# Splitting the last sequence's slot softmax, taking variances from running sums, and re-ranking the last stages of a linear-attention and soft-MoE kernel

## The chip, the cores and the metric

The kernel runs on one core of a Trainium2 chip. A core has five engines that run side by side, each with its own in-order queue: TensorE (PE; its weight loads are shown apart as PEld), VectorE (DVE), ScalarE (ACT), GpSimd (POOL) and SyncE (SP), which here issues the DMA transfers. The metric is the device time of one execution in microseconds (us). Lower is better.

## The reference

The input x holds 4 sequences of 2048 tokens with 256 channels, float32. One layer of linear attention and one soft mixture of experts follow each other, each with a residual and a layer norm behind it:

```python
q, k, v = (gelu(x @ W1 + b1) @ W2 + b2 for each of q, k, v)
scores = tril(q @ k.T / scale)              # no softmax
a = layernorm(scores @ v) * ln_w + ln_b
x = layernorm(x + a)

xn = layernorm(x) * ln_gamma + ln_beta
logits = (xn / norm(xn)) @ (mu / norm(mu))  # 16 experts x 16 slots = 256 columns
dispatch = softmax(logits, over the 2048 tokens of a sequence)
combine = softmax(logits, over the 256 slots)
slot_in = dispatch.T @ xn                   # 256 slots x 256 channels, per sequence
slot_out = gelu(slot_in @ w1 + b1) @ w2 + b2    # per expert
x = layernorm(x + combine @ slot_out)
```

The softmax over the tokens ties a sequence together: no slot sum is final before the sequence's last logits are known, and no output of a sequence can be formed before its slot outputs.

## The kernel before

The 8192 tokens are cut into 16 groups of 512 tokens, four groups to a sequence; a group is four blocks of 128 tokens. For each group t the program states a series of steps, in three functions: `attend` (projections, causal attention with a carried state), `norms` (the two layer norms in front of the experts and the l2 norm) and `back` (logits, their minima over the tokens in `mx`, the softmax over slots, whose result is turned into `ct`). The sign of the logits is flipped, so minima stand for maxima. After the fourth group of a sequence come `softmaxes` (the shift over all tokens of the sequence: two transposes of `mx`, a reduction, a matmul that spreads the shift over all partitions, a copy `cmb` by ACT, then for each group a subtraction on POOL, L1158, and an exponential on ACT, L1167), `slots` and four times `finish`.

`slots` adds up the 16 blocks of a sequence in PSUM, for each half h of the 256 slots (L1182, which appears as two instructions a block and half, 64 a sequence), divides by the sum of the weights (`si`, L1191 and L1192), transposes (L1203), scales (`siT`, L1212), multiplies with w1 (L1227), copies and transposes again (L1237, L1246), applies the Gelu (`hz`, L1265), multiplies with w2 (L1273) and adds the bias (`so`, L1282). There is one tile `so` for all sequences. `finish` loads `ct` back (SP, four transfers), turns it on DVE, and for each block multiplies it with `so` (L1336, `combine`), adds the residual (L1360 on DVE; in the last sequence every second block by a copy on ACT, L1345, and an addition on POOL, L1352), takes mean and variance by bn_stats and bn_aggr (L536, L537), the root by a power on POOL (L525), a product of two small columns on DVE (L563), centers and scales the block (L574 on ACT, L579 on DVE) and stores the group through SP (L1320). The last group is stored in two halves.

The order in each engine's queue is not the order of statement. A planner (`Plan`) gives every step a length and a rank. It runs a small model of the engines, takes in turn the step that can begin earliest, and where several of one engine can begin at the same time, the one of lowest rank. The rank is a base, set by `plan.begin`, that counts groups (a step that reads PSUM gets 1.5 less). The bases of group t are t for `attend`, t+0.6 for `norms`, t+1.1 for `back`; of a sequence whose last group is t, t+1.4 for `softmaxes`, t+1.7 for `slots`, t+2.6 and up for `finish`. For the third sequence alone `slots` has a rank above all others, so that its matmuls fill what PE has left over:

```python
late = 100.0 if b == B - 2 else 0.0
plan.begin(t + 1.7 + (100.0 if late else 0.0))
so = slots(b)
for i in range(NG):
    plan.begin(t + 2.6 + 0.2 * i + (3.5 if late else 0.0))
    finish(t - NG + 1 + i, so)
```

The emitted program is fixed: at run time each engine works through its queue in that order and waits where an operand is late. Tiles are named by tags with a fixed number of places; `dg` (diagonal and `cmb`) has one place, `cm` (shift) three, `root` sixteen, `xT` two, `lg` (logits) seven.

Of the kernel before, what the change touches and what calls it, by code (L numbers as in the profile page):

```python
# [14 lines left out]
P = 128  # L15
G = 4
LAST = 2
# [29 lines left out]
class Plan:  # L47
# [62 lines left out]
    def run(self):  # L110
# [25 lines left out]
        while left:  # L136
            best = None
            for e, steps in ready.items():
                chosen = None
                for s in steps:  # L140
# [4 lines left out]
                    if s.table and s.table != table[0]:  # L145
                        at += self.TABLE
                    key = (at + self.PATIENCE[e] * s.rank, s.rank, at)
# [60 lines left out]
def kernel(  # L208
# [41 lines left out]
    for tag, n, shape in (  # L250
# [23 lines left out]
        ("root", 16, [G]),  # L274
# [5 lines left out]
        ("cm", 3, [EH]),  # L280
# [259 lines left out]

    def variances(mv):
        return mv[:, :, 1:2].rearrange("p c o -> p (c o)")
# [46 lines left out]
    def spread(col, name):  # L589
# [19 lines left out]
    def unit_mu():  # L609
# [26 lines left out]
        row = spread(mr, "mu")  # L636
# [304 lines left out]
    def norms(t):  # L941
# [16 lines left out]
        st2, mv2 = plan.buffer("st", G), plan.buffer("mv", G)  # L958
        for c in range(G):

            def emit(c=c):
                nc.vector.scalar_tensor_tensor(
                    row[:, c, :C], a[:, c, :], r[:, c : c + 1], row[:, c, :C],
                    ALU.mult, ALU.add,
                )

            plan.step("DVE", 0.42, emit, [(a, [c]), r], [(row, [c])])
            means((row, [c]), st2, mv2, c, lambda c=c: row[:, c, :C])
        ve2, w2 = plan.buffer("ve"), plan.buffer("ve")
# [3 lines left out]
                w2.place, variances(mv2), 1.0 + LN_EPS, LN_EPS * LN_EPS, ALU.mult, ALU.add  # L973
            ),
            [mv2], [w2],
        )
        rr = inv_root(w2, G)
        center_on(row, mv2, rr, ("DVE", "ACT") * 2)
        plan.step(
            "DVE", 0.17,  # L980
            lambda: nc.vector.tensor_scalar_add(ve2.place, variances(mv2), LN_EPS),  # L981
# [5 lines left out]
        def emit():  # L987
# [6 lines left out]
        plan.step(  # L994
            "POOL", _pool(G * C),
            lambda: nc.gpsimd.tensor_tensor(
                by_halves(xn), row[:, :, :C].rearrange("p g (k d) -> p k g d", k=KC), gam_h,
                ALU.mult,
            ),
            [row], [xn],  # L1000
        )
        plan.step(
            "POOL", _pool(G * C),
            lambda: nc.gpsimd.tensor_tensor(by_halves(xn), by_halves(xn), bet_h, ALU.add),
            [], [xn],
        )
# [5 lines left out]
        for c in range(G):  # L1012

            def emit(c=c):
                nc.scalar.activation(
                    squares, by_halves(xn)[:, :, c, :], AF.Square,
                    accum_out=ss[:, c : c + 1],
                )
# [12 lines left out]
    def back(t):  # L1031
# [44 lines left out]
        first = t % NG == 0  # L1076
# [49 lines left out]
    def softmaxes(b):  # L1126
# [20 lines left out]
        row = spread(cm, f"cm_{b}")  # L1147
# [6 lines left out]
        for t in range(b * NG, (b + 1) * NG):  # L1154
            lg = l_tiles[t]
# [15 lines left out]
    def slots(b):  # L1171
# [23 lines left out]
        for t in ts_:  # L1195
            del l_tiles[t]
# [245 lines left out]
```

## Time and profile before

| | |
|---|---|
| median of 3 runs | 671.45 us (670.31 to 672.46) |
| the profiled execution | 673.21 us |
| its span, first to last instruction | 671.5 us |
| mean granted PE clock | 0.994 |
| PE busy | 648.3 us, 97% |
| PEld busy | 482.3 us, 72% |
| DVE busy | 499.5 us, 74% |
| ACT busy | 256.8 us, 38% |
| POOL busy | 296.1 us, 44% |

A stage table of the profile gives, for a stretch of the span, its length and the busy time of each engine in it with the number of instructions. From 584 us on, where the last group's attention is done, PE is busy 74.1 of 87.5 us, DVE 58.3, ACT 37.6 and POOL 34.1.

A line of the timeline gives start, length, engine, source line, operation, output and inputs, and how many such instructions are merged; in brackets stand the idle time of the engine before it and what ended it. A line of the chain of waits gives start, length, engine and source line, merged over neighbours of one kind.

### The profile page before, as it was taken

Reading aid. Unit: us, or ns where it says so; the run is one execution under the profiler, and the core shown is the slowest. Engines: PE = TensorE matmul, PEld = TensorE weight load, DVE = VectorE, ACT = ScalarE, POOL = GpSimd, SP = SyncE. Lnnn points to the kernel's source line nnn. Section 1 sums busy time; section 2 is a strip of 40 time slices with the busy share of each in tenths; the row PEclk is TensorE's granted clock in tenths of the full one; section 3 lists DMA queues with packets and bytes.
Section 4 is the critical chain, followed back from the end, with each engine's and each line's share of the span. In section 5 each row is a group of like instructions: output and inputs, shape, how many; then the busy total and the mean of one; then the engine's idle time right before and its main releaser. Section 6 shows DMA issues by size and latency. Waiting matters only on the chain.

```text
span 671.5 us, 9220 instructions
## 1 busy us (share of the span) xinstructions
PE 648.3 (97%) x2966; PEld 482.3 (72%) x2966; DVE 499.5 (74%) x1319; ACT 256.8 (38%) x540; POOL 296.1 (44%) x305
## 2 busy tenths in 40 slices
PE   6999999999999999999999999999999999999994
PEld 3757586776768877858676877767676868877873
DVE  1438586979797878869786488996877689967396
ACT  3130414334355326130626134623425543434346
POOL 4343616061648514361608307446153844543324
PEclk9999999999999999999999999999999999998998
DMA  8953655886667197637586345985586356100034
GB/s 245 254 119 106 133 94 132 127 159 142 118 139 122 44 176 188 176 82 139 131 127 125 63 95 145 214 189 104 120 156 133 76 113 95 55 1 0 32 95 156
DMA packets 311831, 82.59 MB, mean 123 GB/s; under 512 B 244716, under 2 KB 309544, under 8 KB 311784
## 3 DMA queue, kind: packets, MB, share of 16 engines
q1 hardware_dynamic: 310680, 80.96, 57.2%
q10 hardware_dynamic: 960, 0.80, 0.5%
q8 instruction: 23, 0.38, 0.3%
q0 software_dynamic: 144, 0.26, 0.1%
q14 instruction: 24, 0.20, 0.1%
HBM read 51.00 MB, written 30.99 MB: 122 GB/s over the span
## 4 chain that ended last, share of the span: by engine, by line
PE 91%; DVE 5%; issue 1%; DMA 1%; ACT 1%; POOL 0%; ACTq 0%; DVEq 0%
PE mm L720 24%; PE at L1182 8%; PE at L1336 8%; PE mm L1060 8%; PE at L822 8%; PE mm L770 8%; PE at L905 7%; PE mm L743 7%; PE at L795 4%; PE at L909 4%; PE at L855 1%; PE tp L469 1%; DVE st L536 1%; DMA row<-in_x_dram 1%; ACT row L574 1%
## 5 line engine op out<-in xcount | busy, mean ns | idle before, releaser
L525 POOL TENSOR_TENSOR root<-ve,nhalf 128x4 f32<-128x4 f32 (+1 forms) x49 | 50.6, 1033 | 157.4 <-DVE ve L981 56.8
L730 ACT ACTIVATE hid<-mm,cols_sb 128x512 f32<-128x512 f32 x96 | 65.1, 687 | 141.6 <-PE mm L720 141.1
L574 ACT ACTIVATE row<-row,root,root 128x256 f32<-128x256 f32 x94 | 49.9, 591 | 44.7 <-DVE root L563 44.6
L720 PE MATMUL mm<-xT,W1q_sb 128*128 128x512 f32 x128 | 61.5, 610 | 0.3 <-DVE xT L459 0.3
L905 PE MATMUL at<-state,hid 128*128 128x256 f32 x240 | 61.7, 379 | 0.0
L822 PE MATMUL at<-vt,kt 128*128 128x256 f32 x240 | 61.3, 385 | 0.0
L743 PE MATMUL mm<-both_sb,hid 128*128 128x257 f32 x256 | 59.5, 381 | 1.4 <-DVE kt L753 1.4
L1336 PE MATMUL at<-so,ct 128*128 128x256 f32 x256 | 58.3, 381 | 2.2 <-DVE so L1282 1.6
L720 PE MATMUL mm<-xT,W1v_sb 128*128 128x512 f32 x128 | 59.4, 592 | 0.0
L1060 PE MATMUL mm<-mu_sb,xnT 128*128 128x256 f32 x256 | 59.3, 385 | 0.0
L770 PE MATMUL mm<-W2v_sb,hid 128*128 128x256 f32 x256 | 58.2, 380 | 0.3 <-DVE kt L753 0.3
L720 PE MATMUL mm<-xT,W1k_sb 128*128 128x512 f32 x128 | 57.8, 593 | 0.0
L1182 PE MATMUL at<-row,lg 128*128 128x257 f32 x256 | 56.6, 379 | 0.0
L1110 POOL TENSOR_TENSOR sum<-sum,ss 128x4 f32<-128x4 f32 x16 | 3.8, 237 | 119.1 <-DVE ss L1106 102.5
L1336 PEld LDWEIGHTS at<-so,ct 128*128 128x128 f32 x256 | 47.8, 190 | 11.2 <-DVE so L1282 2.0
L1060 PEld LDWEIGHTS mm<-mu_sb,xnT 128*128 128x128 f32 x256 | 49.3, 194 | 8.7 <-issue 1.4
L743 PEld LDWEIGHTS mm<-both_sb,hid 128*128 128x128 f32 x256 | 48.2, 190 | 9.8 <-DVE kt L753 2.0
L536 DVE BATCH_NORM_STATS2 st<-row 128x6 f32<-128x256 f32 x128 | 53.5, 418 | 1.8
L905 PEld LDWEIGHTS at<-state,hid 128*128 128x128 f32 x240 | 45.5, 190 | 12.1 <-issue 5.7
L770 PEld LDWEIGHTS mm<-W2v_sb,hid 128*128 128x128 f32 x256 | 48.3, 190 | 7.5 <-DVE kt L753 0.9
L948 POOL TENSOR_TENSOR row<-row,rows_sb 128x1024 f32<-128x1024 f32 x16 | 35.2, 2204 | 41.8 <-DMA row<-in_x_dram 27.8
L1182 PEld LDWEIGHTS at<-row,lg 128*128 128x128 f32 x256 | 48.4, 190 | 7.1
(129 smaller groups left out, 1176.4 us busy)
## 6 DMA issues: line engine op xcount, KB each, us to landing
bounce<-xn SPq DMA_DIRECT2D x28, 512.0 KB
row<-in_x_dram SPq DMA_DIRECT2D x16, 512.0 KB
bounce<-kt SPq DMA_DIRECT2D x30, 256.0 KB
kT<-bounce SPq DMA_DIRECT2D x60, 128.0 KB
out_dram<-row SPq DMA_DIRECT2D x15, 512.0 KB
xT<-in_x_dram SPq DMA_DIRECT2D x112, 64.0 KB
xnT<-bounce SPq DMA_DIRECT2D x56, 128.0 KB
ct<-bounce SPq DMA_DIRECT2D x56, 128.0 KB
```

What stands on the lines that cost most here:

```text
L525: nc.gpsimd.tensor_tensor(r[:, :n], v[:, :n], nhalf.to_broadcast([P, n]), ALU.pow)
L536: nc.vector.bn_stats(st[:, c, :], access())
L574: nc.scalar.activation(dst[:, c, :C], dst[:, c, :C], AF.Identity, bias=nm[:, i : i + 1], scale=r[:, i : i + 1],)
L720: nc.tensor.matmul(ph.place, wa[f"W1{n}"][:, k, m * P : (m + 1) * P], xT[:, k, :], start=(k == 0), stop=(k == KC - 1),)
L730: nc.scalar.activation(hid[n][:, m, :], ph.place, AF.Gelu, bias=cols_sb[:, 4 * i + m : 4 * i + m + 1],)
L743: nc.tensor.matmul(pk[:, : C + 1], hid["k"][:, k, c * P : (c + 1) * P], wqk_sb[:, k, :], start=(k == 0), stop=(k == KC - 1),)
L770: nc.tensor.matmul(pv[:, j * C : (j + 1) * C], hid["v"][:, k, (c0 + j) * P : (c0 + j + 1) * P], wa["W2v"][:, k, :], start=(k == 0), stop=( ...
L822: nc.tensor.matmul(pds[:, m * C : (m + 1) * C], kt[:, c, m * P : (m + 1) * P], vt[:, c, :], start=True, stop=True,)
L905: nc.tensor.matmul(po[:, :C], qT[:, k, toks[c]], s[:, k, :], start=(k == 0), stop=False,)
L1060: nc.tensor.matmul(pl[:, j * ES : (j + 1) * ES], xnT[:, k, (c0 + j) * P : (c0 + j + 1) * P], mu_sb[:, k, :], start=(k == 0), stop=(k == KC ...
L1182: nc.tensor.matmul(psi[:, : C + 1], lg[:, c, h * P : (h + 1) * P], row[:, c, :], start=(i == 0 and c == 0), stop=(i == NG - 1 and c == G - 1),
L1336: nc.tensor.matmul(pc[:, :C], ct[:, h, c * P : (c + 1) * P], so_t[:, h, :], start=(h == 0), stop=(h == EH - 1),)
```

## The change

In the last sequence (groups 12 to 15):

- The softmax over the tokens is done in two parts. Behind group 14, `softmaxes` runs over groups 12 to 14 with the minima so far, and `part_sums` adds up their slot sums (24 calls of L1182's kind, 12 for each half) and copies them to SBUF (`kept`, in a place of `xT`). Group 15 has minima of its own. Its shift is the lesser of the two, its subtraction and exponential are done block by block (blocks 0 and 3 on POOL, 1 and 2 on DVE), its slot sums take 8 calls, and the kept sums are scaled by the exponential of the difference of the shifts and added.
- `norms` of group 15 has rank 15.0 instead of 15.6 and `back` 15.3 instead of 16.1. The scaling with gamma and beta of that group goes block by block, two blocks on POOL and two on DVE.
- The third sequence's `slots` has rank 15.6 instead of 112.7 and its four `finish` 16.5, 16.8, 17.1 and 17.4 instead of 17.1, 17.3, 17.5 and 17.7. The last sequence has 15.4 and 16.2 for the early softmax and the early sums, 15.5 for the late softmax (16.4 before), 16.7 for `slots`, and 17.6 to 17.9 for `finish` (17.6 to 18.2 before). The product with w2 is not planned before the tile `so` is free.

In groups 8 to 15 (`finish`) and 14 and 15 (the second layer norm in `norms`), the variance no longer comes from bn_stats. The addition on DVE hands out the row sum as well (`accum_out`), and ACT squares 256 times the difference from the mean, again with a row sum. POOL forms the root and the product with the mean by itself. The addition is on DVE for every block. Centering is on ACT for groups 8 to 10, and mostly on DVE from group 11 on.

The places of `root` go from 16 to 24, those of `cm` from 3 to 6. The new term with `TAIL["table"]` in the planner is zero with the value set, 1.0. The core of the diff:

```diff
+ACCZ = 14
+LASTN = 2
+CENTERS = (('ACT', 'ACT', 'ACT', 'ACT'), ('ACT', 'ACT', 'ACT', 'ACT'), ('ACT', 'ACT', 'ACT', 'ACT'), ('DVE', 'DVE', 'DVE', 'ACT'), ('ACT', 'DVE', 'DVE', 'DVE'), ('DVE', 'DVE', 'ACT', 'DVE'), ('DVE', 'DVE', 'DVE', 'DVE'), ('DVE', 'ACT', 'ACT', 'DVE'))
+SUBTRACT = ('POOL', 'DVE', 'DVE', 'POOL')
+TAIL = {'norms': 0, 'back': 0.3, 'softE': 1.4, 'part': 2.2, 'soft': 0.5, 'slots2': 4.6, 'fin2': [5.5, 0.3], 'slots3': 1.7, 'fin3': [2.6, 0.1], 'table': 1.0}
...
+    def squares_of(src, mv, c, access):
+        def emit():
+            nc.scalar.activation(
+                squares.rearrange("p k d -> p (k d)"), access(), AF.Square,
+                bias=mv[:, c, 0:1], scale=-float(C), accum_out=mv[:, c, 1:2],
+            )
+        plan.step("ACT", 0.6, emit, [src, (mv, [c])], [(mv, [G + c])])
+
+    def root_of(mv, cs, factor, add):
...
+            nc.gpsimd.tensor_scalar(
+                negm[:, :n], mv[:, both, 0:1].rearrange("p c o -> p (c o)"), -1.0 / C, 0.0,
+                ALU.mult, ALU.add,
+            )
+        plan.step("POOL", 0.25, emit, [(mv, cs)], [negm])
...
+            nc.gpsimd.tensor_scalar(
+                r[:, :n], variances(mv)[:, both], factor / float(C) ** 3, 0.0 if tile_ else add,
+                ALU.mult, ALU.add,
+            )
+            if tile_:
+                nc.gpsimd.tensor_tensor(r[:, :n], r[:, :n], add[:, both], ALU.add)
+            nc.gpsimd.tensor_tensor(r[:, :n], r[:, :n], nhalf.to_broadcast([P, n]), ALU.pow)
+            nc.gpsimd.tensor_tensor(nm[:, :n], negm[:, :n], r[:, :n], ALU.mult)
...
-    def softmaxes(b):
+    def softmaxes(groups, before=None):
...
+        less = plan.buffer("cm") if before else None
+        if before:
+            def emit():
+                nc.vector.tensor_tensor(cm.place, cm.place, before.place, ALU.min)
+                nc.vector.tensor_tensor(less.place, cm.place, before.place, ALU.subtract)
+            plan.step("DVE", 0.3, emit, [before], [cm, less])
...
+    def part_sums(groups):
+        kept = plan.buffer("xT", KC)
+        for h in range(EH):
+            psi = slot_sums(groups, h)
+            plan.step(
+                "ACT", _act(C),
+                lambda h=h, psi=psi: nc.scalar.copy(kept[:, h, : C + 1], psi[:, : C + 1]),
+                [psi], [(kept, [h])],
+            )
...
+                if kept:
+                    all_ = kept[:, h, :]
+                    nc.vector.scalar_tensor_tensor(
+                        all_[:, : C + 1], all_[:, : C + 1], less[:, h : h + 1],
+                        psi[:, : C + 1], ALU.mult, ALU.add,
+                    )
...
-            plan.step("PE", 0.6, emit, [hz, arrivals["w2"]], [pso])
+            plan.step("PE", 0.6, emit, [hz, arrivals["w2"]], [pso], holds=[so])
...
+    def finish_by_sums(t, row, ct, so, sq, sc):
...
+        n = LASTN if t == ngroups - 1 else G
         for c0 in range(0, G, n):
             cs = list(range(c0, c0 + n))
             for c in cs:
-                combine(c, row, ct, so, sc, part if part and (c + last) % 2 else None)
-                means((row, [c]), st, mv, c, lambda c=c: row[:, c, :C])
...
+                combine(c, row, ct, so, sc, mv)
+                squares_of((row, [c]), mv, c, lambda c=c: row[:, c, :C])
+            r, nm = root_of(mv, cs, 1.0, se)
+            center_by(row, r, nm, [CENTERS[t - ngroups + 2 * NG][c] for c in cs], c0)
+            store(t, row, cs)
...
+        tail = max(0, b - B + 3)
+        last = t == ngroups - 1
         plan.begin(t)
         attend(t)
-        plan.begin(t + 0.6)
+        plan.begin(t + (TAIL["norms"] if last else 0.6))
         norms(t)
...
-        plan.begin(t + 1.1)
+        plan.begin(t + (TAIL["back"] if last else 1.1))
         back(t)
+        if t == ngroups - 2:
+            early = list(range(t - NG + 2, t + 1))
+            plan.begin(t + TAIL["softE"])
+            cm, _ = softmaxes(early)
+            plan.begin(t + TAIL["part"])
+            kept = part_sums(early)
         if t % NG == NG - 1:
...
+            groups = [t] if tail == 2 else list(range(t - NG + 1, t + 1))
+            plan.begin(t + (TAIL["soft"] if tail == 2 else 1.4))
+            _, less = softmaxes(groups, cm if tail == 2 else None)
+            plan.begin(t + (1.7, TAIL["slots2"], TAIL["slots3"])[tail])
+            so = slots(groups, kept if tail == 2 else None, less)
+            first, by = ((2.6, 0.2), TAIL["fin2"], TAIL["fin3"])[tail]
             for i in range(NG):
-                plan.begin(t + 2.6 + 0.2 * i + (3.5 if late else 0.0))
+                plan.begin(t + first + by * i)
                 finish(t - NG + 1 + i, so)
```

## The prediction

> **What bounds the kernel.** I read the page's busy shares first (PE, which is TensorE, 648.3 of 671.5 us), then the busy time by stage, to find the 23.2 us in which PE is idle, then its timeline and the chain that ended last. About 8 us of the idle time lies in the first 80 us (the first loads) and about 2 us is spread over 80 to 600; the change touches neither. The rest lies in three places. The first is the chain from the third sequence's slot sums to its slot outputs, which here runs beside the last group's logits:
>
> ```profile
> 601.73 0.60 PE L1182 MATMUL at<-row,lg 128*128 128x257 f32 x2
> 602.17 0.27 PE L1203 MATMUL tp<-ident,si 128*128 128x128 f32 x1
> 603.11 0.55 PE L1203 MATMUL tp<-ident,si 128*128 128x128 f32 x3 [0.67 <-DVE si L1192]
> 604.29 1.31 PE L1227 MATMUL mm<-w_sb,siT 128*32 128x128 f32 x32 [0.64 <-DVE siT L1212]
> 606.25 0.66 PE L1246 MATMUL tp<-ident,si 128*128 128x128 f32 x2 [0.64 <-DVE si L1237]
> 606.70 4.90 PE L1060 MATMUL mm<-mu_sb,xnT 128*128 128x256 f32 x16
> 611.53 1.07 PE L1273 MATMUL at<-w_sb,hz 128*32 128x256 f32 x16
> 613.39 0.44 PE L1134 MATMUL tp<-ident,mx 128*128 128x128 f32 x2 [0.79 <-DVE mx L1082]
> ```
>
> In brackets stands the idle time before a group: 0.67+0.64+0.64+0.79 = 2.74 us. The 16 matmuls of L1060 start 4.83 us ahead of their successor; the same 16 took 3.45 us at 585.66. The stages (columns PE, PEld, DVE, ACT, POOL, granted clock, DMA share, GB/s) show why, and the end:
>
> ```profile
> 604.00:606.00 2.00, 1.29 (x32) 0.75 (x32) 1.01 (x3) 1.95 (x5) 0.81 (x2) 0.97 0.00 0
> 606.00:608.00 2.00, 1.75 (x6) 1.51 (x7) 0.68 (x3) 0.95 (x4) 0.45 (x1) 0.50 0.00 0
> 608.00:610.00 2.00, 2.00 (x8) 1.65 (x7) 0.00 (x0) 1.27 (x1) 0.00 (x0) 0.68 0.00 0
> ...
> 648.30:662.40 14.10, 14.07 (x64) 12.07 (x64) 13.19 (x45) 9.80 (x21) 8.11 (x11) 1.00 0.14 51
> 662.40:667.00 4.60, 0.01 (x1) 0.00 (x0) 3.37 (x15) 4.57 (x10) 2.83 (x4) 1.00 0.87 303
> 667.00:671.50 4.50, 0.00 (x0) 0.00 (x0) 0.00 (x0) 0.00 (x0) 0.00 (x0) 0.53 0.68 229
> ```
>
> The clock fell to 0.50 and 0.68 after those gaps. The second place is a wait of 1.56 us before the last 64 matmuls of L1336 at 648.33. The third is the tail: PE is done at 662.4 and the span ends 9.1 us later. Two things fill it. ScalarE (ACT) centers a backlog, as the chain says:
>
> ```profile
> 654.86 6.70 PE at L1336 x31
> 661.56 0.02 issue
> 661.58 0.47 ACT xn L1345
> 662.06 4.42 ACT row L574 x9
> 666.48 0.49 ACTq L1435
> ```
>
> Then the stores drain. The last is issued at 667.04, and from 667 to 670 the DMA engines move 343, 342 and 337 GB/s, 1.02 MB, which is the last three stores (512+256+256 KB) together.
>
> **The change, part by part.** 1. *Order and the split softmax.* The last sequence's slot sums were 64 matmul instructions (13.91 us from 621.34) that had to wait for the last group's logits. 48 of them (10.4 us) now need only groups 12 to 14, so they can lie in the gaps from 602 to 613. Are they ready? Group 14's logits matmuls end at 589.1 and its minima at about 591. From the transposes of the minima to ACT's copy of the shift took 613.39 to 616.55, 3.2 us, so the shift is there at about 594.5; if VectorE (DVE) first does the raised norms of group 15, at about 597. GpSimd (POOL) then subtracts three times 2.36 us, with an exponential of 1.06 us behind each: the first group is ready at 598 to 601, the third at 603 to 606, later where POOL first does group 15's two multiplications (598.24 to 602.9 before). The first two groups alone hold 6.9 us of matmuls, more than all four gaps. I take the whole 2.74 us (bounds 0 and 2.74) and, as PE then stays busy, the slow clock: 4.83-3.45 = 1.38 us on L1060 and 1.31-1.08 = 0.23 on L1227 (against 640.82), 1.6 us (bounds 0 and 1.6).
>
> [...]
>
> The second softmax adds to PE two transposes and two matmuls: 0.22+0.43 us by the starts at 512.87 and 516.52, +0.65. DVE gets a second reduction (0.39), two diagonals (0.5), a minimum and a difference of two columns (0.16 each by L563's small form), two subtractions (0.42 each) and two merges (0.47 each), about 3.3 us; its 8 normalisations, 40 statistics and the like follow under 2. ACT gets a shift copy and two copies of the kept sums (0.37 each) and a small exponential (0.31), 1.4 us. All that lies beside PE, which has cover: from 584 to the start of the last outputs its queue holds two logits blocks 6.9, 0.9 transposes, 13.9 slot sums of the third sequence, 10.4+3.5 of the last, two slot chains 6.2, shifts 1.3, 1.7 transposes of ct and 13.8 outputs of groups 8 to 11: 58.6 us, until 642.6. The last slot outputs are due by the old rows at 606.7 (logits start)+3.5+1.8 (minima)+3.6 (shift)+2.3 (subtract, table, exponential)+3.5+13.0 (635.25 to 648.3) = 634.4, so 8 us of slack. Without that cover each microsecond counts in full. SP's queue gets no new transfer; the loads of ct (four of 128 KB a group) move with the ranks, into stages whose DMA share is near 0.
>
> The wait of 1.56 us stays in kind: one slot-output tile, and DVE's addition (L1282) behind the last small matmuls. Before, L1273 ended at 646.77 and DVE came only at 647.88, after statistics. These are gone, but other work may stand there: -0.3 (bounds -0.8 and +0.4). **PE's end: -2.74-1.6+0.65-0.3 = -4.0, at 658.4.**
>
> 2. *Variances from sums.* For 40 blocks DVE drops bn_stats and bn_aggr (0.418+0.182 us, 24 us in all), takes back 8 additions from ACT and POOL (0.47) and 13 centerings (0.42), and reads 40 accumulators (0.083). ACT gains 40 squares with their accumulator reads (0.42+0.19 by L1015), 24 us, and loses 8 copies (0.47) and 13 centerings (0.59), 11.4 us. Each root costs POOL about four small operations of 0.25 more, 11 times. In the last 13.8 us of PE, DVE now has 16x(0.47+0.08)+12x0.42 = 13.8 us, before 16x0.6+8x0.47+2x0.42 and small ones, about 16.5; ACT 16x0.61+4x0.59 = 12.1, before 8x0.47+14x0.59 and carried work; POOL about 11 in both. No engine exceeds PE, though DVE only just.
>
> [...]
>
> *After the last matmul*: addition with accumulator 0.56 (L1070's pair), square 0.61, POOL 0.28+0.28+0.86+0.21 = 1.63 (starts at 596.63 and 596.91, the two-column power at 663.82 and 665.10), centering 0.59, hand-overs 0.3: 3.7 us, before 4.57 (662.4 to 666.97): -0.9 (bounds 0 and -0.9; the trace has no square with a bias, the nearest is L1093's 0.50+0.19, 0.1 more). *Stores*: with ACT's backlog gone, group 14's 512 KB should be out before the last two. It holds the queue 512 KB/343 GB/s = 1.5 us; the full gain is about 1.3, none if DVE or ACT lag again. I take -0.6.
>
> **Sum.** -4.0-0.9-0.6 = -5.5 on a span of 671.5: 666.0. The profiled run took 673.21, span plus 1.7; the runs shown have a median of 671.45 (670.31 to 672.46), so the difference goes on the median: 666.0. Bounds of the forecast: all at best -2.74-1.6+0.65-0.8-0.9-1.3 = -6.7, 664.7; half the gaps and no gain in stores, about 668.5.
>
> **Rivals.** *The cover comes too late* (0.15): POOL's three subtractions, 7.1 us, share it with group 15's norms, 8.6 us (two roots 2.9, four multiplications and additions of one block 2.7 by L1352, scale factors and the last norm 3.0), so the early sums miss the gaps and run afterwards. For it: POOL has 17 us of work for 18 us. Against: the first two groups suffice. Then +0.65-0.3-0.9-0.6 = -1.2, 670.3 (668.5 to 671). *The tail does not shorten* (0.13): DVE, at 13.8 us of work in 13.8, ends as late as before and the stores bunch: -4.0, 667.5.
> *Slower* (0.10): one mechanism, the last slot outputs late. Each queue is fixed when the program is written; if POOL's three subtractions (7.1 us) stand before group 15's norms, and ACT's 16 squares and 13 centerings of groups 8 to 11 (16x0.54+13x0.59 = 16.3 us) before the exponentials of group 15 and the Gelu of the last slots, PE runs out of filler. All of it is 23.4 us late. It costs from 8 us on, and the kernel is slower by 0.3% from 8+5.5+2 = 15.5 on. With half of ACT's share, 15.3-8 = 7.3, plus the 1.6 us of slow clock again, -5.5: +3.4, 674.9. Against it: ACT is busy only 37.6 of 78.4 us from 584 to 662.4.
>
> **Chances.** Forecast 0.62, tail unchanged 0.13, late cover 0.15, slower 0.10. About 0.3%, 2 us, is what a measurement here can tell from no change. Faster by more: 0.62+0.13 and a third of the late cover, 0.80; within: 0.10; slower: 0.10. The range goes from 664.0 (the best sum, less the scatter of the runs) to 671.0, which leaves out the slower case and little else.
>
> **What would show it.** Right: L1182 matmuls between 602 and 613 with no idle time over 0.3 us before them and a granted clock of 1.00; PE ends near 658; under 8.5 us from there to the end; under 4 us from the last matmul to the last centering. Wrong: idle PE before the last L1336 block over 2 us, naming ACT's Gelu or POOL's subtraction; or the last three stores again within 1 us of each other.

## The result and the profile after

| | before | after |
|---|---|---|
| median | 671.96 us (670.31 to 672.7, 4 runs) | 665.68 us (665.13 to 666.1, 4 runs) |
| ratio | | 0.9909 (0.9888 to 0.9930) |
| the profiled execution, its span | 673.21, 671.5 us | 665.13, 663.4 us |
| group 14's logits begin | 585.66 us | 583.85 us |
| from there to PE's end | 76.75 us | 72.18 us |
| from PE's end to the span's end | 9.09 us | 7.37 us |
| PE busy | 648.3 us, 97% | 646.1 us, 97% |
| DVE, ACT, POOL busy | 499.5, 256.8, 296.1 us | 488.5, 269.2, 299.6 us |
| mean granted PE clock | 0.994 | 0.998 |

The medians differ by 6.3 us, the two profiled spans by 8.1, since the profiled execution before was the slowest of its runs and the one after the fastest. 1.8 us of the 8.1 lie ahead of group 14's logits: 0.3 in the first load, 0.83 in a wait for DVE near 287 us that is not there after, the rest in small pieces. At least the first two are not the change's doing: up to there both kernels work through the same order on every engine, and a kernel that differs from the changed one only behind 655 us (the last of the experiments) has the wait again (0.8 us) and begins group 14's logits at 584.96 instead of 583.85. So an execution differs from the next by a microsecond ahead of the changed part. All comparisons below count from the start of group 14's logits (L1060 before, L1165 after). From there to the end it is 85.84 us before and 79.55 after: -6.3 us.

The places that the prediction names, first in PE's timeline of the changed kernel (start, length, engine, source line, operation, tiles, number; in brackets the idle time of PE before it and what ended it). L1310 is the slot sums, L1165 the logits, L1240 the transposes of the minima (L1187 on DVE), L677 the spread of the shift, L1362, L1386, L1405 and L1432 the slot chain, L1515 the outputs. On the other engines L1276 is the subtraction of the shift, L1288 the exponential, L1424 the Gelu, L1523 the addition with the row sum, L557 the squares, L581 to L588 the steps of the root on POOL, L603 and L608 the centering on ACT and DVE:

```profile
599.03 0.70 PE L677 MATMUL mm<-dg,ones 128*128 128x256 f32 x2 [0.46 <-DVE dg L671]
...
601.30 3.62 PE L1165 MATMUL mm<-mu_sb,xnT 128*128 128x256 f32 x16
604.75 2.77 PE L1310 MATMUL at<-row,lg 128*128 128x257 f32 x12
607.36 0.60 PE L1362 MATMUL tp<-ident,si 128*128 128x128 f32 x4
607.80 0.60 PE L1310 MATMUL at<-row,lg 128*128 128x257 f32 x2
608.43 0.44 PE L1240 MATMUL tp<-ident,mx 128*128 128x128 f32 x2
608.71 1.47 PE L1310 MATMUL at<-row,lg 128*128 128x257 f32 x6
610.11 1.08 PE L1386 MATMUL mm<-w_sb,siT 128*32 128x128 f32 x32
...
640.58 1.07 PE L1432 MATMUL at<-w_sb,hz 128*32 128x256 f32 x16
641.77 14.26 PE L1515 MATMUL at<-so,ct 128*128 128x256 f32 x64
```

Slot sums now stand between the steps of the chain, and from 599.03 to the end of the chain at 618.6 no idle time of 0.2 us or more is left but the 0.46. The 16 logits matmuls start 3.45 us ahead of their successor instead of 4.83. Between the last small matmuls, which end at 641.65, and the last outputs there is 0.12 us, where before PE was idle for 1.56 us. The stages of the changed kernel from 598 us on (length, then PE, PEld, DVE, ACT, POOL busy with counts, granted clock, DMA share, GB/s):

```profile
598.00:614.00 16.00, 15.50 (x101) 12.64 (x100) 10.02 (x29) 8.07 (x21) 10.43 (x9) 1.00 0.00 1
614.00:641.80 27.80, 27.68 (x188) 22.64 (x187) 14.36 (x50) 17.69 (x50) 5.71 (x17) 1.00 0.22 41
641.80:656.00 14.20, 14.20 (x64) 11.88 (x64) 11.43 (x41) 12.44 (x38) 7.47 (x22) 1.00 0.41 143
656.00:660.20 4.20, 0.03 (x1) 0.00 (x0) 2.55 (x9) 2.19 (x6) 3.07 (x9) 1.00 0.69 238
```

In the stage of the chain PE is busy 15.50 of 16 us at full clock, before 13.24 at 0.89. In the last 64 outputs the DMA engines move 143 GB/s instead of 51, so stores leave that used to pile up; the last three are issued over 2.3 us instead of 1.0 (the last at 660.21), and behind the issue of the last one remain 3.2 us instead of 4.5. The chain that ended last (start, length, engine and line) runs through POOL:

```profile
655.88 0.21 POOL root L581
...
656.16 0.21 POOL root L586
...
656.43 0.83 POOL root L587
...
658.58 0.69 POOL root L587
...
659.58 0.60 ACT row L603
```

Before, ACT's backlog of nine centerings stood there. Now it is the roots of the last group's two halves, one behind the other on POOL.

### The profile page after: what moved, and what is told of

The parts are those of the page before. It is cut to its first block, busy times and chain, and to the rows that moved or that the text cites. A ratio compares the mean times of both kernels' runs of the same rounds, so it can differ in the third digit from the quotient of the medians.

```text
span 663.4 us, 9351 instructions
## 1 busy us (share of the span) xinstructions
PE 646.1 (97%) x2970; PEld 481.1 (73%) x2970; DVE 488.5 (74%) x1290; ACT 269.2 (41%) x604; POOL 299.6 (45%) x350
## 4 chain that ended last, share of the span: by engine, by line
PE 90%; DVE 6%; DMA 1%; issue 1%; POOL 1%; ACT 0%; ACTq 0%; POOLq 0%; DVEq 0%
PE mm L796 23%; PE mm L846 8%; PE at L898 8%; PE at L1310 8%; PE mm L819 8%; PE at L1515 8%; PE mm L1165 8%; PE at L981 7%; PE at L871 4%; PE at L985 4%; PE at L931 2%; DMA both_sb<-in_W2q_dram 1%; DVE mx L1187 1%; DVE st L547 1%; PE tp L480 1%
## 5 line engine op out<-in xcount | busy, mean ns | idle before, releaser
L536 POOL TENSOR_TENSOR root<-ve,nhalf 128x4 f32<-128x4 f32 x38 | 39.9, 1051 | 124.8 <-DVE ve L1031 49.6
L1515 PE MATMUL at<-so,ct 128*128 128x256 f32 x256 | 58.1, 381 | 0.8 <-DVE row L1523 0.6
L1310 PE MATMUL at<-row,lg 128*128 128x257 f32 x256 | 58.2, 380 | 0.0
L1165 PE MATMUL mm<-mu_sb,xnT 128*128 128x256 f32 x256 | 58.0, 379 | 0.0
L1515 PEld LDWEIGHTS at<-so,ct 128*128 128x128 f32 x256 | 47.9, 190 | 10.1 <-issue 1.7
L1165 PEld LDWEIGHTS mm<-mu_sb,xnT 128*128 128x128 f32 x256 | 48.4, 190 | 8.3 <-issue 1.4
L1310 PEld LDWEIGHTS at<-row,lg 128*128 128x128 f32 x256 | 48.0, 190 | 7.1 <-issue 0.4
L898 PEld LDWEIGHTS at<-vt,kt 128*128 128x128 f32 x240 | 44.4, 190 | 12.1 <-issue 5.4
L940 ACT COPY cs<-at 128x256 f32<-128x256 f32 (+1 forms) x16 | 5.9, 372 | 108.0 <-PE at L931 108.0
```

The source lines that it names most:

```text
L536: nc.gpsimd.tensor_tensor(r[:, :n], v[:, :n], nhalf.to_broadcast([P, n]), ALU.pow)
L898: nc.tensor.matmul(pds[:, m * C : (m + 1) * C], kt[:, c, m * P : (m + 1) * P], vt[:, c, :], start=True, stop=True,)
L1165: nc.tensor.matmul(pl[:, j * ES : (j + 1) * ES], xnT[:, k, (c0 + j) * P : (c0 + j + 1) * P], mu_sb[:, k, :], start=(k == 0), stop=(k == KC ...
L1310: nc.tensor.matmul(psi[:, : C + 1], lg[:, c, h * P : (h + 1) * P], row[:, c, :], start=(i == 0), stop=(i == n - 1),)
L1515: nc.tensor.matmul(pc[:, :C], ct[:, h, c * P : (c + 1) * P], so_t[:, h, :], start=(h == 0), stop=(h == EH - 1),)
```

## The experiments

All kernels are timed beside the kernel before in the same session; its median was 671.4 us in the first four, 671.3 in the next four and 671.1 in the last four. The stretches are those of the profiled execution, as in the table above: one execution each, and the one of the kernel before took 673.21 us, 1.3 us above that kernel's median in the table and 1.8 to 2.1 above those of the later sessions.

| kernel | median us | ratio to before | logits to PE's end | PE's end to the end |
|---|---|---|---|---|
| before | 671.96 | 1 | 76.75 | 9.09 |
| after | 665.68 | 0.9909 (0.9888 to 0.9930) | 72.18 | 7.37 |
| before, six matmuls in the gaps | 671.0 | 0.9996 (0.9987 to 1.0005) | 75.50 | 9.14 |
| after without the split | 676.06 | 1.0071 (1.0058 to 1.0085) | 82.43 | 7.34 |
| after with bn_stats, additions on DVE | 675.53 | 1.0064 (1.0051 to 1.0078) | 75.05 | 13.69 |
| after with bn_stats, as before | 674.1 | 1.0034 (1.0013 to 1.0054) | 73.92 | 12.78 |
| after with the old ranks | 677.3 | 1.0086 (1.0072 to 1.0100) | 81.86 | 8.65 |
| split alone | 675.78 | 1.0075 (1.0055 to 1.0096) | 75.78 | 13.25 |
| new ranks alone | 680.55 | 1.0143 (1.0123 to 1.0162) | 83.38 | 10.4 |
| sums alone | 684.5 | 1.0205 (1.0181 to 1.0229) | 92.04 | 7.4 |
| sums alone, no table term in the planner | 670.75 | 0.9996 (0.9979 to 1.0013) | 75.57 | 7.9 |
| after, sums in groups 12 to 15 only | 668.18 | 0.9961 (0.9948 to 0.9974) | 72.06 | 9.96 |
| after, group 15 not in blocks | 674.07 | 1.0039 (1.0019 to 1.0059) | 81.5 | 7.5 |
| after, last roots partly on DVE | 666.04 | 0.9935 (0.9921 to 0.9949) | 72.15 | 7.8 |

**The slow clock by itself.** The kernel before, with two needless matmuls ahead of each of the three steps of the third sequence's chain. They fill the gaps and do nothing else.

```diff
+        def fill(to, n):
+            for _ in range(n if b == B - 2 else 0):
+                nc.tensor.matmul(to, ident, b2_sb[:, 0, :], start=True, stop=True)
...
+            fill(pst[:, :C], 2)
...
+            fill(pht[:, :C], 2)
...
+            fill(phh[:, :C], 2)
```

> The kernel before with six needless matmuls (two instructions each, 0.43 us) in the third sequence's slot chain, two before each of the three small steps, into banks that the next step overwrites; nothing else is changed. They turn idle PE into busy PE without doing its work. If short gaps lowered the clock: the granted clock stays 1.00 from 604 to 610, the 16 logits matmuls take about 3.45 us instead of 4.83, and the kernel gains about 1.4 us less what the fillers overrun (0.2 us each, 0.6): 0.5 to 1.5 us, 670.5 to 671.5. [...]

PE's timeline of this kernel (L1202 holds the needless matmuls, L1280 is the product with w2), and one of its stages, in the columns of above:

```profile
606.14 1.13 PE L1202 MATMUL tp<-b_sb,ident 128*128 128x256 f32 x4
...
607.33 3.62 PE L1060 MATMUL mm<-mu_sb,xnT 128*128 128x256 f32 x16
610.88 1.07 PE L1280 MATMUL at<-w_sb,hz 128*32 128x256 f32 x16
```

```profile
606.00:608.00 2.00, 2.00 (x18) 1.62 (x11) 0.79 (x3) 0.98 (x2) 1.03 (x1) 1.00 0.00 0
```

The granted clock stays at 1.00 where it was 0.50, and the 16 logits matmuls start 3.55 us ahead of their successor instead of 4.83. PE ends 1.25 us earlier, counted from group 14's logits, although it does six matmuls more. So in these two executions the low clock went with the gaps, and cost about that much. In the timed runs only -0.3 us is left (-0.9 to +0.3), which can't be told from nothing.

The runs suggest why: not every execution of the kernel before had the low clock. The mean granted clock of its 54 runs in these three sessions goes from 0.992 to 0.997; the 23 with 0.995 or less have a median of 672.1 us, the 31 others one of 671.0. The profiled one had 0.994, this kernel's 11 runs 0.995 to 0.997. Where in the span the clock was low, the runs don't say. And the same waits are not always followed by slow matmuls. Two kernels of below (the sums alone, first as they are, then without the table term) run PE through the same matmuls with the same two waits of 1.57 and 1.14 us within 3.82 and 3.77 us (from the end of L1405 to the start of L1432), PE at work for 1.11 and 1.06 us of these, and the 16 small matmuls behind them take 1.94 us in the one and 1.07 in the other (the mean granted clock of the two executions was 0.987 and 0.997):

```profile
614.19 1.94 PE L1432 MATMUL at<-w_sb,hz 128*32 128x256 f32 x16
```

```profile
612.77 1.07 PE L1432 MATMUL at<-w_sb,hz 128*32 128x256 f32 x16
```

So neither the length of the waits nor PE's busy share settles it; what does, no run here shows.

**One part taken away.** Three kernels undo one of the three parts of the change each. First the split:

```diff
-        if t == ngroups - 2:
+        if False:
...
-            groups = [t] if tail == 2 else list(range(t - NG + 1, t + 1))
+            groups = list(range(t - NG + 1, t + 1))
```

> The changed kernel without the split of the last softmax: groups 12 to 15 share one minimum, one shift and one run of slot sums, as before; the new ranks, the squares on ACT and the block-by-block work on group 15 stay. If the early slot sums are what fills the gaps (my theory): the gaps and the slow clock of the first slot chain return for the most part (2.74 + 1.6 us) and 0.65 us of shift work goes, so 665.7 + 3.7 = about 669.4 us, PE idle and at a clock under 0.8 somewhere between 600 and 612, the tail from PE's end to the end of the span still about 7.4 us. Rival, the freed VectorE gives the gain by itself: 665.5 to 666.5 us and no new idle PE.

```profile
614.66 10.95 PE L1310 MATMUL at<-row,lg 128*128 128x257 f32 x36 [4.86 <-ACT lg L1288]
625.54 0.64 PE L1432 MATMUL at<-w_sb,hz 128*32 128x256 f32 x8
```

This timeline of PE shows more than the return of the gaps. With the new ranks the last sequence's sums stand ahead of the third sequence's last small matmuls (L1432), so PE waits 4.86 us for exponentials that can only follow group 15, with nothing behind them to fill in. PE's end moves by 10.3 us, not by the 3 to 4 of the gaps and the clock. Both the theory and its rival were short of that: without the split the new ranks cost more than they bring.

Then the variances, put back to bn_stats and bn_aggr, and with them the roots and the centering (on ACT, in the last group on DVE and ACT by turns); all additions stay on DVE:

```diff
-ACCZ = 14
+ACCZ = 99
...
-        if t >= ngroups - 2 * NG:
-            finish_by_sums(t, row, ct, so, sq, sc)
-            return
...
+                combine(c, row, ct, so, sc)
+                means((row, [c]), st, mv, c, lambda c=c: row[:, c, :C])
...
+            center_on(row, mv, inv_root(ve, n), ("DVE", "ACT") if last else ("ACT",) * G, c0)
```

> The changed kernel with variances by bn_stats and bn_aggr again in groups 8 to 15 (centering as before: ACT, and DVE and ACT by turns in the last group), all additions on DVE; split and new ranks stay. My theory: PE's end moves by less than 1 us, the tail goes back from 7.4 to 9 us or, as DVE has 8 additions more than before, to 10 or 11: 667.5 to 669 us. Rival, the freed VectorE gives the whole gain: 671 us or more, with idle PE before the last outputs.

The time, 675.5 us, is that of the rival, but most of the loss lies in the tail and not in idle PE: PE ends 2.9 us later than in the changed kernel and the tail takes 13.69 us, the longest of all. 1.66 us of PE's loss is a wait for group 15's minima, of which more at the end. As the kernel before spread half of these additions over ACT and POOL, a second one does so too, which leaves the last outputs as they were but for the places of the copies (the edit is shown against the last kernel):

```diff
+            part = plan.buffer("pt")
...
-                combine(c, row, ct, so, sc)
+                combine(c, row, ct, so, sc, part and (c + last) % 2)
```

> The changed kernel with the variances and the last outputs exactly as before: bn_stats, bn_aggr, every second block of the last sequence added through ACT and POOL (with two small places of their own); split and new ranks stay. u2 put all 16 additions on DVE, which by itself costs 8 x 0.47 us. My theory: PE's end stays within 1 us of the changed kernel's and the tail goes back to 9 or 10 us: 667.5 to 669 us. Rival: split and ranks only work with a freed DVE, so this stays near u2, 673 to 676 us, with a tail over 11 us.

The stages of this kernel, up to the last outputs, beside them, and behind PE's end:

```profile
621.90:644.10 22.20, 22.08 (x152) 18.48 (x150) 18.57 (x57) 6.31 (x13) 2.02 (x2) 1.00 0.24 49
644.10:658.20 14.10, 14.10 (x64) 11.91 (x64) 13.05 (x45) 8.87 (x19) 7.99 (x11) 1.00 0.31 111
658.20:667.00 8.80, 0.02 (x1) 0.00 (x0) 5.18 (x24) 5.73 (x12) 3.83 (x5) 0.74 0.40 140
```

PE's stretch is 2.8 us shorter than before, and the kernel is still slower than before by 0.1 to 0.5%. DVE is busy 18.57 of 22.2 us ahead of the last outputs and 13.05 of 14.1 beside them, and carries 5.18 us of work behind PE's end (2.55 in the changed kernel); ACT waits 2.57 us for a root from DVE and then centers ten blocks in a row, and the tail is 12.78 us. This is the rival again: an earlier end of PE is worth nothing here unless DVE gets there with it.

Third, the old ranks:

```diff
-        plan.begin(t + (TAIL["norms"] if last else 0.6))
+        plan.begin(t + 0.6)
...
-        plan.begin(t + (TAIL["back"] if last else 1.1))
+        plan.begin(t + 1.1)
...
-            plan.begin(t + (TAIL["soft"] if tail == 2 else 1.4))
+            plan.begin(t + 1.4)
...
-            plan.begin(t + (1.7, TAIL["slots2"], TAIL["slots3"])[tail])
+            plan.begin(t + (1.7, 101.7, 1.7)[tail])
```

> The changed kernel with the old ranks for norms and back of group 15, the third sequence's slots and finish, the late softmax and the last finish; split and squares stay. With rank 112.7 the third sequence's slot sums stand behind the early and the late sums of the last sequence, so its chain to the slot outputs comes when little is left to fill it. My theory (the cover must be in the right order): 669 to 674 us with idle PE of 3 us or more between 600 and 645. Rival, the ranks matter little once the sums are split: 665.5 to 666.5 us.

Slower than either theory had it. PE waits 3.6 us for the exponentials, 1.6 for a centered block, 1.5 for the slot sums to be divided, and ends 9.7 us later than in the changed kernel.

**One part alone.** The same three parts, each put on the kernel before by itself. The split alone is the changed kernel with two of the edits above together, the variances as before with the additions spread, and the old ranks:

> The kernel before with the split softmax (and the block-by-block work on group 15) alone: old ranks, variances and last outputs as before. As in u3, the early sums stand ahead of the third sequence's slot sums, whose chain is then uncovered: 674 to 678 us. Rival, u3 was slow because of the squares on ACT: 668 to 671 us.

As expected, slower: by 4.5 us (3.7 to 6.4 from the interval). PE's stretch is 1.0 us shorter than before, the tail 4.2 us longer (13.25). The new ranks alone, with the wait of the product with w2 for `so`:

```diff
-    plan.begin(t + 0.6)
+    plan.begin(t + (0.0 if t == ngroups - 1 else 0.6))
...
-    plan.begin(t + 1.7 + (100.0 if late else 0.0))
+    plan.begin(t + (4.6 if late else 1.7))
```

> The kernel before with the new ranks alone (group 15's norms and back, the third sequence's slots and finish, the late softmax, the wait for the one slot-output tile). Without early sums there is nothing to put into the gaps: 671 to 674 us, idle PE of 2.5 us or more between 600 and 616. Rival, the ranks bring a good part of the gain by themselves: under 669.5 us.

Slower by 1.4%, well beyond what was expected. PE waits 2.9 us for slot outputs, 2.2 for the minima and 1.1 for the Gelu, and runs 16 outputs in 5.00 us (from 615.43) that take 3.45 in the kernel without blocks of below (from 621.05). The sums alone (the split, the blocks of group 15 and the new ranks undone):

> The kernel before with the squares on ACT and the roots on POOL alone; order, ranks and the undivided softmax as before. My theory: the gaps of 2.74 us and the slow clock stay, the tail shrinks by 1 to 2.3 us: 669 to 670.5 us. Rival, the three parts need each other, as u1 to u3 suggest: no gain at all or a loss, 671 to 675 us.

The slowest kernel of all, at 1.0205, and a miss: theory and rival ended at 675 us. PE's timeline, and after it ACT's, of this kernel:

```profile
640.32 5.04 PE L1310 MATMUL at<-row,lg 128*128 128x257 f32 x12 [7.76 <-ACT lg L1288]
```

```profile
618.42 0.51 ACT L557 ACTIVATE squares<-row,mv 128x256 f32<-128x256 f32 x1 [3.75 <-DVE row L1523]
...
626.37 4.04 ACT L603 ACTIVATE row<-row,root,root 128x256 f32<-128x256 f32 x8
...
635.24 2.66 ACT L603 ACTIVATE row<-row,root,root 128x256 f32<-128x256 f32 x5
637.91 1.28 ACT L1288 ACT_TABLE_LOAD   x1
639.21 3.89 ACT L1288 ACTIVATE lg<-lg 128x1024 f32<-128x1024 f32 x4
```

POOL had done the last subtraction at 624.06. The exponentials come at 639.21, behind 16 squares and 13 centerings (618.42 to 637.90), and PE runs dry for 7.76 us. This is the prediction's slower rival to the letter, ACT's part of it: squares and centerings of groups 8 to 11 ahead of the exponentials that PE needs. Why does the planner put them there? The exponential needs another table than the Gelu ahead of it (the load of 1.28 us at 637.91), so in the planner's model, where such an exchange takes 1.3 us, it begins that much later than a square that is ready, and loses each time. Without that term in the choice:

```diff
-TAIL = {..., 'table': 1.0}
+TAIL = {..., 'table': 0.0}
```

> v2 (squares on ACT alone) with one number changed in the planner, TAIL table 0.0 for 1.0: a step that needs a table load on ACT is no longer put back behind those that do not. In v2 the four exponentials stood behind 16 squares and 13 centerings, and PE waited 7.8 us for them. If that place in ACT's queue is the cause: the wait falls under 2 us and the time to 672 to 677 us. Rival, POOL's subtractions or the missing cover are the cause: 682 us or more.

ACT's timeline with the table term at zero:

```profile
613.27 1.28 ACT L1288 ACT_TABLE_LOAD   x1
...
622.69 1.06 ACT L1288 ACTIVATE lg<-lg 128x1024 f32<-128x1024 f32 x1
```

The last exponential starts at 622.69 instead of some 642, the wait is gone, and the median falls by 13.75 us. One term of the planner thus moves more than twice what the whole change brings. The same kernel also says what the sums are worth in this order: in the profiled execution the tail is 7.9 us instead of 9.1, with PE's stretch 1.2 us shorter (the 16 logits matmuls start 3.56 us ahead of their successor there instead of 4.83), and in the timed runs nothing (0.9979 to 1.0013).

**How much relief is needed.** The changed kernel, with sums in the last sequence only; groups 8 to 11 also center on ACT again, group 11 with four blocks instead of one:

```diff
-        if t >= ngroups - 2 * NG:
+        if t >= ngroups - NG:
```

> The changed kernel with the squares on ACT for the last sequence only; groups 8 to 11 take bn_stats and bn_aggr again and center on ACT. v1 ended with DVE and ACT still busy for 5.2 and 5.7 us after PE. If it is DVE's work over both sets of last outputs that decides (theory): 16 x 0.6 us more on DVE in a stretch of 21.7 us where it was busy 13.4, so it falls behind by 1 to 3 us and the tail grows by as much: 667 to 669.5 us. Rival, only the last sequence's statistics matter: 665.2 to 666.3 us.

The stage of the last outputs and the one behind it, then ACT and DVE, and ACT's last square:

```profile
641.80:656.50 14.70, 14.58 (x76) 11.93 (x66) 13.32 (x53) 11.18 (x32) 5.98 (x14) 1.00 0.28 87
656.50:666.50 10.00, 0.04 (x1) 0.00 (x0) 3.07 (x10) 4.44 (x13) 4.47 (x13) 0.60 0.70 242
```

```profile
645.03 0.51 ACT L557 ACTIVATE squares<-row,mv 128x256 f32<-128x256 f32 x1 [4.49 <-DVE row L1523]
...
656.58 0.48 DVE L1523 SCALAR_TENSOR_TENSOR row<-at,sum,row 128x256 f32<-128x256 f32 x1
...
659.08 0.19 ACT L557 ACTIVATION_READ_ACCUMULATOR squares<-row,mv 128x1 f32 x1
```

PE's stretch is the changed kernel's within 0.1 us (72.06), the tail 2.6 us longer. So groups 8 to 11, whose last matmuls stand ahead of the last 64, still set the tail, and the time is as expected. The way is not quite the expected one. DVE, with their statistics, works 13.32 us of the 14.7 (11.43 of 14.2 in the changed kernel) and is late at first: ACT stands idle for 4.49 us until an addition is done. But DVE catches up, and its last addition starts 0.04 us behind PE's end. What ends last is ACT, which from 645.03 on has no pause, eight centerings of groups 10 and 11 (4.1 us) between its squares, and is through with them 2.7 us behind PE (1.2 in the changed kernel); POOL's roots follow. As group 11's centering moved to ACT with the same edit, this kernel doesn't tell DVE's share from ACT's.

**Group 15 in blocks.** The changed kernel with one subtraction, one exponential and one scaling for all of group 15:

```diff
-            n = 1 if t == ngroups - 1 else G
+            n = G
...
-        for c in range(G) if t == ngroups - 1 else ():
+        for c in ():
...
-        if t < ngroups - 1:
+        if True:
```

> The changed kernel with group 15 not split by blocks: gamma and beta on POOL for the whole group, one subtraction and one exponential. My theory gave the chain of group 15 a slack of 8 us; this lengthens it by 2 to 4 us: 665.3 to 667 us. Rival, the order hangs on it as on the other parts: 669 us or more, with PE waiting for the late exponentials.

A clear miss: I held these blocks for a matter of 2 us at most, inside the slack, and the median is 8.4 us above the changed kernel's; the rival was right that the order hangs on them, though PE waits for the Gelu and not for the exponentials. PE's timeline and ACT's:

```profile
647.90 1.94 PE L1432 MATMUL at<-w_sb,hz 128*32 128x256 f32 x16 [5.77 <-ACT hz L1424]
649.76 16.15 PE L1515 MATMUL at<-so,ct 128*128 128x256 f32 x64
```

```profile
611.46 1.28 ACT L1424 ACT_TABLE_LOAD   x1
...
614.46 1.28 ACT L1296 ACT_TABLE_LOAD   x1
...
643.25 2.65 ACT L603 ACTIVATE row<-row,root,root 128x256 f32<-128x256 f32 x5
645.92 1.28 ACT L1424 ACT_TABLE_LOAD   x1
647.22 0.63 ACT L1424 ACTIVATE hz<-hp 64x128 f32<-64x128 f32 x2
```

And ACT's in the changed kernel:

```profile
614.51 0.42 ACT L1288 ACTIVATE lg<-lg 128x256 f32<-128x256 f32 x1
614.95 1.28 ACT L1424 ACT_TABLE_LOAD   x1
...
636.12 0.62 ACT L1424 ACTIVATE hz<-hp 64x128 f32<-64x128 f32 x2
```

In the changed kernel the last exponential just precedes the one table load for the Gelu, and the last sequence's Gelu at 636.12 finds its table there. With one large exponential the third sequence's Gelu comes first, the exponential needs its table back, and the last Gelu needs a third load. DVE had made `hp` at 637.75; the planner put eight squares and five centerings, 7.8 us from 638.07 on, ahead of the load, and the Gelu came at 647.22. Behind the wait the 16 small matmuls take 1.94 us instead of the changed kernel's 1.07, and the last 64 outputs 16.15 instead of 14.26. Here the blocks are worth the order that they lead the planner to, not the latency that they save.

**The end of the chain.** For the last group, the negated mean and the sum of variance and constant go from POOL to DVE:

```diff
-            r, nm = root_of(mv, cs, 1.0, se)
+            r, nm = root_of(mv, cs, 1.0, se, t == ngroups - 1)
...
+                nc.vector.scalar_tensor_tensor(
+                    r[:, :n], variances(mv)[:, both], factor / float(C) ** 3, add[:, both],
+                    ALU.mult, ALU.add,
+                )
```

> The changed kernel with two of POOL's small operations for the last group moved to DVE (minus the mean; variance plus its constant in one operation instead of two), the power and the product stay on POOL. At the end POOL's roots stand one behind the other from 653.9 to 659.5 us. If they set the end: the last centering comes 0.5 to 0.8 us earlier, 664.9 to 665.3 us by the median, tail under 6.9 us in the profile. Rival, DVE's own centerings stand in front of the moved operations: no gain, 665.5 to 666.5 us, tail 7.2 us or more.

The timeline of all engines, behind PE's end at 657.11:

```profile
657.56 1.06 DVE L632 TENSOR_SCALAR row<-row,root,root 128x256 f32<-128x256 f32 x3
...
658.53 0.16 DVE L580 TENSOR_SCALAR root<-mv 128x2 f32<-128x2 f32 x1
...
659.16 0.69 POOL L598 TENSOR_TENSOR root<-root,nhalf 128x2 f32<-128x2 f32 x1 [2.36 <-DVE root L580]
```

As in the rival, the moved operations stand behind DVE's centerings, and POOL waits 2.36 us for them. Nothing is gained (666.04 against 665.68 in another session, the intervals overlap). No kernel tried beats the changed one.

## Why the prediction was right

It said 666.0 us; the median is 665.68. Part of that closeness is luck. The forecast drop was 5.5 us, set on a median of 671.45 over three runs; the median over four is 671.96, and the drop 6.3. (In the three later sessions the kernel before measured 671.1 to 671.4, so 6.3 may be 0.6 to 0.8 too much.) Of its four signs of being right one failed: from the last matmul to the last centering it takes 4.15 us, not under 4. (PE's end at 656.03 is near the 658 only with the 1.8 us ahead of group 14's logits.) The terms, each from group 14's logits on, from one profiled execution of each kernel:

- *Gaps in the third sequence's chain*, -2.74: of 2.74 us one gap of 0.46 is left, so -2.28. The early sums were in time, so the rival of late cover did not happen.
- *Slow clock*, -1.6: 4.83 to 3.45 and 1.31 to 1.08, so -1.61 as forecast, with two reservations. The 0.23 of L1227 is not the clock: from 604.29 to 605.60 the granted clock before was 1.00, and in three other kernels (new ranks alone, sums alone with and without the table term) the same 32 matmuls take 1.31 or 1.32 us behind the same wait of 0.64, though the 16 logits matmuls behind them take 3.72 us there and not 4.90. It goes away with the wait; why it comes with it, no run shows. And the 1.38 is what the profiled execution had; the medians hold less of it where the clock did not fall, as the kernel with needless matmuls and the clocks of the runs suggest. In the profiled executions the clock fell to 0.50 behind gaps of at most 0.67 us, and stayed at 1.00 where needless matmuls filled them.
- *More work on PE*, +0.65: PE's busy time fell by 0.87 us (72.43 to 71.56); with the 1.61 just named, 0.74 was added.
- *The wait before the last outputs*, -0.3 with bounds of -0.8 and +0.4: it went from 1.56 to 0.12, -1.44, outside the bounds. The step that was mis-sized is "These are gone, but other work may stand there". Nothing took their place: DVE's addition starts 0.02 us after the first half of the small matmuls ends (641.27 to 641.29), where before statistics ran until 647.88, 1.1 us past the end of all of them.
- *PE's end*, -4.0: -2.28-1.61+0.74-1.44 = -4.6; the stretch is shorter by 4.57.
- *After the last matmul*, 4.57 to 3.7: it became 4.15 (656.03 to 660.18), half of the 0.9. The path was costed as if the last half of the last group had POOL to itself. In the chain its root stands behind the other half's, and POOL's small operations beside DVE's centerings took up to 0.35 us instead of 0.19.
- *Stores*, -0.6 with bounds of 0 and -1.3: from the last issue to the end 4.46 became 3.19, -1.27, the whole of it.

So the single errors, +0.5, +0.1, -1.1, +0.5 and -0.7, nearly cancelled, and the stretch from group 14's logits to the end fell by 6.3 us instead of 5.5. DVE's work was counted rightly: beside PE's last 14.2 us and in the 4.2 behind, it works 11.43+2.55 = 14.0 us, against 13.8. The accumulators cost little beyond the 0.08 us of reading them, which was counted: beside PE's last outputs the addition with one takes 0.484 us in the median (17 of L1523), without it 0.474 before (L1360). With two sources in SBUF and an accumulator, the additions in group 14's and 15's norms (L1041) took 0.475 to 0.486 us, as long as the one with a source in PSUM.

Two things in the argument fell, though the time did not depend on them. The sum was made as if each term could be had by itself. Each part alone made the kernel slower (split +4.5, ranks +9.3, sums +13.2 us), and taking away any one left it slower than before by 2.8 to 5.9 us. And the 8 us of slack for the last slot outputs were counted in durations; in the changed kernel's trace 3.8 are left (the last Gelu ends at 636.74, PE comes to the product with w2 at 640.58). What decides is the fixed order: the rival was one table load away, as the sums alone and the kernel without blocks show (waits of 7.76 and 5.77 us). Nothing in the profile of before told which way the planner would fall, so the 0.10 for it rested on little.

What stays open: how often the clock falls in the kernel before, and so how much of the 1.38 us is in the medians; which of the ranks carry the gain, as only all of them were undone together; and what the table term is worth in the changed kernel, which was not tried.

## What to carry to other kernels

Where a list scheduler fixes the queues, the parts of a retuned tail don't add up: read the emitted order on the engine that gets the moved work, above all what stands behind a change of ACT's table (1.28 us each here). A gain at the end of the bound engine counts only if the engines that finish its work get there too, so take their load over the last two stages, not only the last. And short gaps on PE can cost twice, once as idle time and again in the clock behind them (2.74 and 1.38 us in the profiled execution before); the granted clock of the stage tells whether they did, and one execution doesn't tell it of the next.

## What the runs showed of the hardware

- The granted clock fell to 0.50 (606 to 608 us in the kernel before) behind three gaps of 0.64 to 0.67 us within 3.81 us (602.44 to 606.25), with PE at work for 1.84 us of these, and stayed at 1.00 in the execution in which needless matmuls filled them. Behind the same two waits of 1.57 and 1.14 us the 16 small matmuls took 1.94 us in one kernel and 1.07 in another, and behind the single wait of 1.56 us at 648.33 in the kernel before the clock stayed at 1.00.
- A minimum of two SBUF tiles on DVE, 0.42 us in the median, took up to 2.47 us beside a subtraction of 2.49 on POOL. In the kernel with bn_stats and all additions on DVE, PE waits 1.66 us for group 15's minima, which DVE takes while POOL subtracts the shift from groups 12 to 14. A line of the view by tile (number, then shortest, median and longest in ns, first and last start), and the timelines of POOL and DVE:

```profile
L1187 DVE TENSOR_TENSOR mx<-mx,lg x54: 414/422/2471, 98.2 to 607.3; 128x256 f32<-128x256 f32 x54
```

```profile
601.99 7.46 POOL L1276 TENSOR_TENSOR lg<-lg,dg 128x1024 f32<-128x1024 f32 x3 [0.28 <-ACT dg L1265]
```

```profile
606.72 3.01 DVE L1187 TENSOR_TENSOR mx<-mx,lg 128x256 f32<-128x256 f32 x2
```

The last two minima take 3.01 us instead of twice the usual 0.42, and end 0.28 us behind POOL's third subtraction (609.45). In the changed kernel two of group 15's three minima are slow beside the early subtractions: the first takes 1.16 us, the last two 1.64 together. In the kernel with the new ranks alone two of its minima take 0.88 us (607.81) while POOL stands idle. But not every one beside a subtraction is slow: in the kernel with bn_stats and all additions on DVE the first, at 604.29, took 0.42. So the early subtractions may have a price in group 15's own chain, 0.74 and 0.80 us over the usual, that the prediction did not count; what holds the minima, no run shows.
- Reading an accumulator takes 0.08 us on DVE and 0.19 on ACT, an exchange of ACT's table 1.28 us (83, 187 and 1283 ns in the rows DVE_READ_ACCUMULATOR, ACTIVATION_READ_ACCUMULATOR and ACT_TABLE_LOAD of the changed kernel).
